# A graph layer on one core: TensorE's loop turned at another place, one more memset ahead of the left-over edges, and a dst block on another queue

## The chip, the core and the metric

The kernel runs on one core of a Trainium2 chip. The metric is the device time of one execution in microseconds. Five engines work side by side, each in the order of its own instruction list: TensorE (PE; the profile shows its weight loads as PEld), VectorE (DVE), ScalarE (ACT), GpSimd (POOL) and SyncE (SP). An engine waits for another one by semaphores only. SyncE, ScalarE and GpSimd also issue DMAs, each on a queue of its own; the transfers share 16 DMA engines.

## The reference

`x` has 12,500 nodes of 128 values, `edge_attr_48` 412,500 edges of 48 values, sorted by their destination `dst`. `src` and `batch` (all zeros) play no part in the result beyond one row of globals.

```python
h   = relu(layernorm(x))                                  # no scale, no shift
agg = segment_sum(edge_attr_48, dst, num_segments=12500)  # 48 values for a node
z   = concat([h, agg, graph_globals[0]])                  # 128 + 48 + 64
out = x + relu(z @ W1 + b1) @ W2 + b2                     # 256 hidden values
```

Everything is float32. Read and written in all: 79 MB of edges, 6.4 MB of x, 6.4 MB of result.

## The kernel before

**Edges into nodes.** The sorted edges are cut into chunks of 768 (128 partitions of 6 edges), and 4 chunks make a group. For a group VectorE builds one-hot tiles (`oh`: which of 28 neighbouring nodes an edge belongs to) and TensorE multiplies them with the edges (`su`, line 681), which gives the group's sums by node offset in a PSUM bank S0 or S1; ScalarE copies them out (`ss`, line 685). A second, wider one-hot (`pl`, 186 nodes, line 668) places them into the aggregate of 1,024 nodes in two PSUM banks (`pc`, line 703).

**Stages.** One iteration handles 11 groups of edges and 1,024 nodes; there are 12 iterations. The 11 groups lie in six slots: slots 0 to 3 and 5 hold two groups each, slot 4 one. Each slot has one buffer `e[s]` for its edges; once its sums are done, the loads for the next iteration (`le`, 576 KB for a group) go out on SyncE's queue, in the order of the sums. The nodes come in two blocks A and B of 512: x is loaded on ScalarE's queue (`lx`), VectorE computes the statistics (`st`, line 710), ScalarE normalizes (`xn`, line 731), TensorE transposes (`tu`, line 740), then come the first layer (`hh`, `ha`, lines 750 and 755), ScalarE's ReLU (`hi`, line 760) and, in the next iteration, the second layer (`w2`, line 776). VectorE adds the residual and keeps the result in SBUF (`ho` into `hold`, line 780), and only behind that does GpSimd compute x + b2 for the current block (`xb`, line 735), into the buffer that `ho` has just read. The load of the next x waits for `xb`, as it overwrites x.

**Order.** A class `Flow` collects all operations with the names that they read and write. From these names it derives the waits: an operation that writes a name waits for whoever wrote or read it before. On one engine the operations stand in the order in which the program lists them. TensorE's part of an iteration is, in order: sums of slots 0, 1, 2; placing of slot 5 (first half), 0 and 1; second layer of A and B; sums of slots 3, 4, 5; transposes; placing of slots 2, 3, 4 and 5 (second half); first layer. For TensorE alone the loop does not turn where an iteration begins, but ahead of the operation that `f.mark` names, here `su4`: between the sums of slots 3 and 4.

**Start.** SyncE issues the loads of the five blocks of `dst` (`ld`, lines 524 to 529; the last block has 25 full rows and one row that is filled by two small DMAs), then those of the first edges. ScalarE fills some buffers with zeros before it copies the transposed dst blocks (line 597).

**End.** After the loop, in `epilogue`, 5 full chunks and one of 84 edges are left over, and 212 nodes. `load_rest` puts the chunks into slot 0's buffer with two DMAs on SyncE's queue: `lez` (720 KB, writes the names `e0.0` and `e0.1`) and `lezt` (the 84 edges, 14 partitions; writes `e0.1` and `ezt`). Behind them on the same queue stand the 22 stores of the held results (`soh`, 256 KB each, line 786), then the stores of the last blocks A and of the left-over nodes; block B's last store is on ScalarE's queue. The left-over sums are `sur` (line 938), which for the chunk of 84 edges uses 14 rows only.

Of the kernel before, what the change touches and what calls it, by code (L numbers as in the profile page):

```python
# [18 lines left out]
P = 128  # L19
EPS = 1e-5  # L20
T = 6
CE = P * T
CG = 4
# [3 lines left out]
IN = 1024  # L27
# [7 lines left out]
V = 28  # L35
NV = 32
SLOTS = [(1, 6), (2, 7), (3, 8), (4, 9), (5,), (10, 11)]
NS = len(SLOTS)
# [367 lines left out]
def kernel(  # L406
# [12 lines left out]
    nc = tc.nc  # L419
    N, D = x.shape  # L420
    E, DE = edge_attr.shape
# [6 lines left out]
    TAIL = E - NFULL * CE  # L428
# [81 lines left out]
    op = f.op  # L510
    A, B, Z = 0, 1, 2

    def dma(eng, name, reads, writes, dst_ap, src_ap):
        def emit(i):
            with nc.allow_non_contiguous_dma(reason="small pieces"):
                return [f.of[eng].dma_start(dst_ap(i) if callable(dst_ap) else dst_ap, src_ap(i) if callable(src_ap) else src_ap)]  # L516
        op(eng, name, reads, writes, emit, dma=True)

    def load_dst(b):
        rows = min(P, NCH - b * P)  # L520
        full = min(P, NFULL - b * P)
        d = di[b]
        k = f"di{b}"
        dma("SP", f"ld{b}", [], [k], d[:full], dst[b * P * CE:(b * P + full) * CE].rearrange("(c e) -> c e", e=CE))
        if full < rows:
            n = CE // TAIL
            dma("SP", f"ld{b}r", [], [k + "r"], d[full:rows, :n * TAIL].rearrange("a (n e) -> a n e", e=TAIL),
                dst[None, None, E - TAIL:E].to_broadcast([1, n, TAIL]))
            dma("SP", f"ld{b}s", [], [k + "s"], d[full:rows, n * TAIL:], dst[None, E - TAIL:E - TAIL + CE - n * TAIL])

    def span(ap, i, a, n):
        return ap[ds(a(i), n)] if not isinstance(i, int) else ap[a(i):a(i) + n]
# [137 lines left out]
    def onehots(s):  # L670
        g = SLOTS[s]
        onehot(s, oh[s], ["rel_i"], rel_i[:, g[0] - 1:g[0]] if len(g) == 1 else rel_i[:, g[0] - 1:g[1]:g[1] - g[0]])
# [13 lines left out]

    def sums(s):
        m = len(SLOTS[s])
        add_up(s, s % 2, oh[s], e[s], ss[s], [f"e{s}.{j}" for j in range(m)], m * CG)

    def place(s, fresh=(), part=None):

# [36 lines left out]
    def norm(k, m=P):  # L729
        op("ACT", f"xn{k}", [f"x{k}", f"x{k}t", f"sc{k}", f"sh{k}"], [f"xn{k}"], lambda i: [  # L730
            nc.scalar.activation(xn[k][:m, r], xt[k][:m, r], AF.Relu, bias=sh[k][:m, r:r + 1], scale=sc[k][:m, r:r + 1]) for r in range(RR[k])])  # L731
# [56 lines left out]
    def prologue():  # L788
# [1 line left out]
        for b in range(NB):  # L790
            load_dst(b)
        dma("SP", "le5.1", [], ["e5.1"], e[5][:, CG:], edge_attr[:GE].rearrange("(c p t) d -> p c (t d)", p=P, t=T))
        for s in range(NS):
            if s == 2:
                load_x(A, lambda i: 0, eng="SP")
                load_x(B, lambda i: BN, eng="SP")
            for k in (0, 1):
                if (s, k) != (5, 1) and k < len(SLOTS[s]):
                    load_e(s, 1, k)
# [40 lines left out]
        for b in range(NB):  # L840
# [21 lines left out]
        places(1)  # L862
        op("DVE", "spare", [], ["spare"] + [f"di{b}" for b in range(NB)] + [f"di{NB - 1}r", f"di{NB - 1}s"] + [f"df{k}" for k in range(DF)],
           lambda i: [nc.vector.memset(hold[0][:, 0:1], 0.0)])
        for s in (3, 4, 5):
            onehots(s)
        for s in (2, 3, 4):
            places(s)
# [2 lines left out]
    def body(it):  # L871
        f.at = it

        def add_slots(*some):
            for s in some:
                sums(s)
                if it < NIT - 1:
                    load_e(s, 1)

        keep = lambda i: (i + NIT - 2) % (NIT - 1)  # L880
        farthest()
        fetch(1)
        add_slots(0, 1)
        for k in (A, B):
            stats(k)
            variance(k)
        add_slots(2)
        onehots(0)
        shift(A)
        shift(B)  # L890
        onehots(1)
        onehots(2)
        norm(A)
        norm(B)
        place(5, (0,), 0)
        place(0, (1,))
        place(1)
        places(5)
        fetch_off(1)
        places(0)  # L900
        places(1)
        for k in (A, B):
            second(k, P, ph[k], f"PH{k}", keep)
        for k in (A, B):
            add_b(k)

        add_slots(3, 4, 5)
        for s in (3, 4, 5):
            onehots(s)
        turn(A)  # L910
        turn(B, P, po, "PO")
        if it < NIT - 1:
            load_x(A, lambda i: (i + 1) % NIT * IN)
            load_x(B, lambda i: (i + 1) % NIT * IN + BN)
        for s in (2, 3, 4):
            place(s)
        place(5, (), 1)
        sums_out(A)
        sums_out(B)
        for s in (2, 3, 4):  # L920
            places(s)
        layers(layer_x)
        layers(layer_e)
        layers(relu)

    def epilogue():
        f.at = NIT
        m = RN // RZ
        load_rest()
        store_held()  # L930
        add_b(Z, m)
        stats(Z, m)
        variance(Z, m)
        shift(Z, m)
        norm(Z, m)
        rest = lambda j, c: P if j * CG + c < FULL else TP
        op("PE", "sur", ["oh0", "oh1", "e0.0", "e0.1", "ezt"], ["S0"], lambda i: [
            nc.tensor.matmul(S[0][NV * c:NV * c + V, j * DE:(j + 1) * DE], oh[j][:rest(j, c), c * T + t], e[0][:rest(j, c), j * CG + c, t * DE:(t + 1) * DE],  # L938
                             start=(t == 0), stop=(t == T - 1), skip_group_check=True)
            for j in range(2) for t in range(T) for c in range(min(CG, RC - j * CG))])  # L940
        op("ACT", "ssr", ["S0"], ["ssr"], lambda i: [nc.scalar.copy(ssr.rearrange("p j d -> p (j d)"), S[0][:, :2 * DE])])
        place(5, (0,), 0)
        turn(Z, m, S[1], "S1")
        verdict_0()
        verdict_1()
        todo = [(j,) + v for j, g in enumerate((1, 2)) for v in pieces(g)]
        op("PE", "pcr", ["ssr", "pl0", "pl1"], ["bk0"], lambda i: [
            nc.tensor.matmul(agg[bk][:DE, at:at + w], ssr[:, j], pl[j][:, 0, frm:frm + w], start=False, stop=True, skip_group_check=True)
            for j, bk, at, frm, w in todo])
        sums_out(Z, m)  # L950
        zr = [S[0][:, a * RN:(a + 1) * RN].rearrange("p (r c) -> p r c", r=RZ) for a in range(NH)]
        for a in range(NH):
            layer_x(f"z{a}", "S0", zr[a], Z, a, a == 0, m)
        for a in range(NH):
            layer_e(f"z{a}", "S0", zr[a], Z, a, m)
        for a in range(NH):
            relu(f"z{a}", "S0", zr[a], Z, a, m)
        second(A, P, ph[A], "PH0")
        store(A, lambda i: (i - 1) * IN)
        verdict_2()  # L960
        second(B, P, ph[B], "PH1")
        store(B, lambda i: (i - 1) * IN + BN, eng="ACT")
        second(Z, m, pt, "PT")
        store(Z, lambda i: i * IN, m)
        for e_ in f.of:
            op(e_, f"rb{e_}", ["bad"], [], lambda i, e_=e_: [f.of[e_].reg_load(flag_of[f.of[e_].engine], bad[0:1, 0:1])])
# [8 lines left out]
    ends = [f"ot{k}" for k in range(3)] + [f"x{k}" for k in (A, B)] + [f"hold{k}.{j}" for k in (A, B) for j in range(NIT - 1)]  # L975
    op("SP", "end", [], ends, lambda i: [nc.sync.nop(nofuse=True)])
    f.order((0, NIT - 1))
    f.mark = "su4"
    tc.mark_branch_hint_location("skip", engines=[ET.PE, ET.DVE])
    with tc.tile_critical(no_gpsimd_drain=True):  # L980
        f.run()
# [33 lines left out]
```

## Time and profile before

| | us |
|---|---|
| median of 3 runs | 277.77 (277.67 to 277.8) |
| the profiled execution | 277.39 |
| its span, first to last instruction | 275.6 |
| TensorE busy | 252.7 (92%) |
| VectorE busy | 239.5 (87%) |
| ScalarE busy | 128.2 (47%) |
| GpSimd busy | 54.5 (20%) |

The DMA moved 94.33 MB at a mean of 342 GB/s over the span.

How to read it: the span is shown in 40 equal slices of 6.9 us, and a digit is the busy share of a slice in tenths. A row of the timeline gives the start and the duration in us, the engine (a q behind it means that the engine only issues), the line of the kernel, the operation, the tile written and the tiles read, the shapes, how many instructions in a row it stands for, and in brackets how long the engine was idle before it and what ended that. A row of the windows gives the stretch, its length, then for PE, PEld, DVE, ACT and POOL busy time and number of instructions, and at the end TensorE's granted clock, the DMA's share and GB/s. A row of the DMA view gives tile written, tile read, queue, count, KB, and the us from issue to landing. A row of the waits gives who waited for what: us in total, times, the longest.

### The profile page before, as it was taken

The numbers are of one execution on the slowest core, as the hardware profiler recorded it, in microseconds if no ns is written. First come the engines' busy times: TensorE is split into PE (matmuls) and PEld (weight loads), VectorE is DVE, ScalarE is ACT, GpSimd is POOL, SyncE is SP. The second block draws the span as 40 slices with busy tenths as digits, with TensorE's granted clock in tenths as the row PEclk, the third lists the DMA queues.
The fourth block names the chain that finished last, engine by engine and source line by source line (L and its number), as shares of the span: only waits on it lengthen the run. The fifth ranks groups of instructions, "written<-read, shape, count | busy, mean of one in ns | idle before, by whom it ended". The sixth has DMA issues, their size and how long they took to land.

```text
span 275.6 us, 17205 instructions
## 1 busy us (share of the span) xinstructions
PE 252.7 (92%) x7567; PEld 195.6 (71%) x7568; DVE 239.5 (87%) x591; ACT 128.2 (47%) x316; POOL 54.5 (20%) x47
## 2 busy tenths in 40 slices
PE   2946999999999999999999999999999999999990
PEld 2946866867858849859768768578498497597580
DVE  4899997998989989989989979989899899799521
ACT  7800544535437337245445355373373463454520
POOL 8100050040220400500500502304105005007000
PEclk9955999999999999999999999999999999999999
DMA  6999999999999999999999999999999999995992
GB/s 213 297 363 356 341 357 362 356 357 361 356 361 357 356 362 356 356 362 356 356 362 356 356 362 356 359 359 356 362 357 356 362 356 356 362 356 208 368 363 73
DMA packets 79012, 94.33 MB, mean 342 GB/s; under 512 B 3227, under 2 KB 72189, under 8 KB 78998
## 3 DMA queue, kind: packets, MB, share of 16 engines
q1 hardware_dynamic: 75398, 87.63, 96.1%
q10 hardware_dynamic: 3312, 6.03, 6.2%
q0 software_dynamic: 288, 0.49, 0.7%
q8 instruction: 7, 0.11, 0.2%
q14 instruction: 7, 0.06, 0.1%
HBM read 87.75 MB, written 6.40 MB: 342 GB/s over the span
## 4 chain that ended last, share of the span: by engine, by line
PE 87%; SPq 5%; DMA 3%; issue 2%; DVE 0%
PE s L681 27%; PE ph L776 18%; PE ph L750 8%; PE ax L703 7%; SPq L516 5%; PE ph L755 5%; PE po L750 4%; PE pt L750 4%; PE pt L755 4%; DMA e<-in_edge_attr_dram 3%; PE ay L703 3%; PE pt L740 3%; PE po L740 2%; PE s L938 1%; PE s L750 0%
## 5 line engine op out<-in xcount | busy, mean ns | idle before, releaser
L662 DVE TENSOR_TENSOR oh<-iota_v,rel_i 128x1344 f32<-128x1344 f32 (+1 forms) x78 | 130.8, 1716 | 0.0
L681 PEld LDWEIGHTS s<-e,oh 128*28 128x28 f32 x6336 | 75.1, 109 | 23.3 <-issue 21.4
L681 PE MATMUL s<-e,oh 128*28 128x48 f32 x6336 | 80.9, 210 | 11.0 <-issue 6.7
L735 POOL TENSOR_TENSOR xba<-xa,b_sb 128x512 f32<-128x512 f32 x12 | 15.4, 1285 | 198.3 <-DVE holda L780 198.3
L685 ACT COPY ss<-s 128x96 f32<-128x96 f32 (+1 forms) x72 | 16.8, 234 | 70.6 <-PE s L681 70.6
L668 DVE TENSOR_SCALAR pl<-iota_w,off_i 128x186 f32<-128x186 f32 x141 | 35.1, 309 | 0.5
L735 POOL TENSOR_TENSOR xbb<-xb,b_sb 128x512 f32<-128x512 f32 x12 | 31.1, 2591 | 0.0
L760 ACT ACTIVATE hida<-ph,bias 128x512 f32<-128x512 f32 x12 | 8.2, 687 | 42.2 <-PE ph L755 42.2
L703 PE MATMUL ax<-pl,ss 128*48 128x186 f32 (+3 forms) x172 | 27.1, 300 | 0.0
L776 PEld LDWEIGHTS ph<-w,hida 128*128 128x128 f32 x208 | 24.2, 191 | 3.8 <-issue 3.8
L776 PE MATMUL ph<-w,hida 128*128 128x128 f32 x208 | 26.7, 281 | 0.0
L703 PE MATMUL ay<-pl,ss 128*48 128x186 f32 (+3 forms) x168 | 26.3, 297 | 0.0
L776 PE MATMUL ph<-w,hidb 128*128 128x128 f32 x208 | 25.6, 276 | 0.6 <-issue 0.6
L776 PEld LDWEIGHTS ph<-w,hidb 128*128 128x128 f32 x208 | 24.3, 192 | 0.8 <-issue 0.7
L731 ACT ACTIVATE xna<-xa,sha,sca 128x128 f32<-128x128 f32 x48 | 19.8, 482 | 5.1 <-DVE sha L727 5.1
L710 DVE BATCH_NORM_STATS2 sta<-xa 128x6 f32<-128x128 f32 x48 | 10.5, 281 | 12.1 <-DMA xa<-in_x_dram 12.1
L703 PEld LDWEIGHTS ax<-pl,ss 128*48 128x48 f32 x172 | 17.6, 126 | 4.3 <-issue 2.0
L731 ACT ACTIVATE xnb<-xb,shb,scb 128x128 f32<-128x128 f32 x48 | 19.6, 479 | 0.0
L703 PEld LDWEIGHTS ay<-pl,ss 128*48 128x48 f32 x168 | 17.8, 124 | 0.0
L755 PE MATMUL ph<-ags,w1a 48*128 48x512 f32 x48 | 13.5, 641 | 0.0
L750 PE MATMUL ph<-hta,w1h 128*128 128x512 f32 x24 | 13.5, 644 | 0.0
L750 PE MATMUL ph<-htb,w1h 128*128 128x512 f32 x24 | 12.3, 592 | 0.0
(150 smaller groups left out, 301.5 us busy)
## 6 DMA issues: line engine op xcount, KB each, us to landing
e<-in_edge_attr_dram SPq DMA_DIRECT2D x133, 576.0 KB, 10.0
xa<-in_x_dram ACTq DMA_DIRECT2D x11, 256.0 KB, 5.8
xb<-in_x_dram ACTq DMA_DIRECT2D x11, 256.0 KB, 6.3
out_dram<-holda SPq DMA_DIRECT2D x11, 256.0 KB, 3.2
out_dram<-holdb SPq DMA_DIRECT2D x11, 256.0 KB, 3.3
holda<-in_dst_dram SPq DMA_DIRECT2D x4, 384.0 KB, 4.9
e<-in_edge_attr_dram SPq DMA_DIRECT2D x1, 720.0 KB, 8.9
xa<-in_x_dram SPq DMA_DIRECT2D x1, 256.0 KB, 10.5
```

Of the source, the lines that this page charges most:

```text
L516: return [f.of[eng].dma_start(dst_ap(i) if callable(dst_ap) else dst_ap, src_ap(i) if callable(src_ap) else src_ap)]
L662: op("DVE", f"oh{name}", reads + ["iota_v"], [f"oh{name}"], lambda i: [nc.vector.tensor_tensor(ov, iota_v[:, None, None, :].to_broadcast([ ...
L668: nc.vector.tensor_scalar(out[:, j], iota_w, o[j], None, OP.is_equal) for j in range(len(o))])
L681: nc.tensor.matmul(S[k][NV * c:NV * c + V, j * DE:(j + 1) * DE], o[:, (j * CG + c) * T + t], ev[:, j * CG + c, t * DE:(t + 1) * DE], start ...
L685: op("ACT", f"ss{name}", [f"S{k}"], [f"ss{name}"], lambda i: [nc.scalar.copy(sv.rearrange("p j d -> p (j d)"), S[k][:, :m * DE])])
L703: out.append(nc.tensor.matmul(agg[bk][h:h + DE, at:at + w], sv[:, j], pv[:, j, frm:frm + w], start=bk in fresh and bk not in seen, stop=Tr ...
L731: nc.scalar.activation(xn[k][:m, r], xt[k][:m, r], AF.Relu, bias=sh[k][:m, r:r + 1], scale=sc[k][:m, r:r + 1]) for r in range(RR[k])])
L735: nc.gpsimd.tensor_tensor(xb[k][:m], xt[k][:m], b2_sb[:m, None, :].to_broadcast([m, RR[k], D]), OP.add)])
L740: op("PE", f"tu{k}", [f"xn{k}", "ident"], [key], lambda i: [nc.tensor.transpose(pv[:, r, :m], xn[k][:m, r], ident[:m, :m]) for r in range( ...
L750: nc.tensor.matmul(o, w1h[:, a * P:(a + 1) * P], hT[k][:, :, :m], start=first, stop=False, skip_group_check=True)])
L755: nc.tensor.matmul(o, w1a[h:h + DE, a * P:(a + 1) * P], ag[k // 2][h:h + DE, :, :m], start=False, stop=True, skip_group_check=True)])
L776: nc.tensor.matmul(ov[:m, r], hid[k][:, a, r, :m], w2[:, a], start=(a == 0), stop=(a == NH - 1)) for r in range(RR[k]) for a in range(NH)])
```

## The change

- In the loop the sums of slot 4 move from behind those of slot 3 into the first burst, behind slot 2; slot 3 takes S0 and slot 4 S1. The load of slot 4 for the next iteration and its one-hot move with it (and in the prologue the order of loads and one-hots follows). `f.mark` becomes `su3`, so that TensorE's loop turns behind the second layer, ahead of the sums of slot 3.
- The three DMAs of the last dst block are issued on ScalarE's queue instead of SyncE's.
- In the epilogue a memset `ezz` on GpSimd zeroes e[0]'s last chunk (128x288), listed ahead of `load_rest` and writing the name `e0.1`. The left-over sums then use all 128 rows for each chunk.
- In the epilogue the verdict on VectorE (a test whether the windows sufficed), the second layer of block A and its store move ahead, to just behind the left-over sums.

```diff
--- before.py
+++ after.py
@@ -521,12 +521,13 @@
         full = min(P, NFULL - b * P)
         d = di[b]
         k = f"di{b}"
-        dma("SP", f"ld{b}", [], [k], d[:full], dst[b * P * CE:(b * P + full) * CE].rearrange("(c e) -> c e", e=CE))
+        eng = "SP" if full == rows else "ACT"
+        dma(eng, f"ld{b}", [], [k], d[:full], dst[b * P * CE:(b * P + full) * CE].rearrange("(c e) -> c e", e=CE))
         if full < rows:
             n = CE // TAIL
-            dma("SP", f"ld{b}r", [], [k + "r"], d[full:rows, :n * TAIL].rearrange("a (n e) -> a n e", e=TAIL),
+            dma(eng, f"ld{b}r", [], [k + "r"], d[full:rows, :n * TAIL].rearrange("a (n e) -> a n e", e=TAIL),
                 dst[None, None, E - TAIL:E].to_broadcast([1, n, TAIL]))
-            dma("SP", f"ld{b}s", [], [k + "s"], d[full:rows, n * TAIL:], dst[None, E - TAIL:E - TAIL + CE - n * TAIL])
+            dma(eng, f"ld{b}s", [], [k + "s"], d[full:rows, n * TAIL:], dst[None, E - TAIL:E - TAIL + CE - n * TAIL])
 
     def span(ap, i, a, n):
         return ap[ds(a(i), n)] if not isinstance(i, int) else ap[a(i):a(i) + n]
@@ -686,7 +687,7 @@
 
     def sums(s):
         m = len(SLOTS[s])
-        add_up(s, s % 2, oh[s], e[s], ss[s], [f"e{s}.{j}" for j in range(m)], m * CG)
+        add_up(s, {3: 0, 4: 1}.get(s, s % 2), oh[s], e[s], ss[s], [f"e{s}.{j}" for j in range(m)], m * CG)
 
     def place(s, fresh=(), part=None):
 
@@ -790,7 +791,7 @@
         for b in range(NB):
             load_dst(b)
         dma("SP", "le5.1", [], ["e5.1"], e[5][:, CG:], edge_attr[:GE].rearrange("(c p t) d -> p c (t d)", p=P, t=T))
-        for s in range(NS):
+        for s in (0, 1, 2, 4, 3, 5):
             if s == 2:
                 load_x(A, lambda i: 0, eng="SP")
                 load_x(B, lambda i: BN, eng="SP")
@@ -862,7 +863,7 @@
         places(1)
         op("DVE", "spare", [], ["spare"] + [f"di{b}" for b in range(NB)] + [f"di{NB - 1}r", f"di{NB - 1}s"] + [f"df{k}" for k in range(DF)],
            lambda i: [nc.vector.memset(hold[0][:, 0:1], 0.0)])
-        for s in (3, 4, 5):
+        for s in (4, 3, 5):
             onehots(s)
         for s in (2, 3, 4):
             places(s)
@@ -884,12 +885,13 @@
         for k in (A, B):
             stats(k)
             variance(k)
-        add_slots(2)
+        add_slots(2, 4)
         onehots(0)
         shift(A)
         shift(B)
         onehots(1)
         onehots(2)
+        onehots(4)
         norm(A)
         norm(B)
         place(5, (0,), 0)
@@ -904,8 +906,8 @@
         for k in (A, B):
             add_b(k)
 
-        add_slots(3, 4, 5)
-        for s in (3, 4, 5):
+        add_slots(3, 5)
+        for s in (3, 5):
             onehots(s)
         turn(A)
         turn(B, P, po, "PO")
@@ -926,6 +928,7 @@
     def epilogue():
         f.at = NIT
         m = RN // RZ
+        op("POOL", "ezz", [], ["e0.1"], lambda i: [nc.gpsimd.memset(e[0][:, FULL], 0.0)])
         load_rest()
         store_held()
         add_b(Z, m)
@@ -933,16 +936,17 @@
         variance(Z, m)
         shift(Z, m)
         norm(Z, m)
-        rest = lambda j, c: P if j * CG + c < FULL else TP
         op("PE", "sur", ["oh0", "oh1", "e0.0", "e0.1", "ezt"], ["S0"], lambda i: [
-            nc.tensor.matmul(S[0][NV * c:NV * c + V, j * DE:(j + 1) * DE], oh[j][:rest(j, c), c * T + t], e[0][:rest(j, c), j * CG + c, t * DE:(t + 1) * DE],
+            nc.tensor.matmul(S[0][NV * c:NV * c + V, j * DE:(j + 1) * DE], oh[j][:, c * T + t], e[0][:, j * CG + c, t * DE:(t + 1) * DE],
                              start=(t == 0), stop=(t == T - 1), skip_group_check=True)
             for j in range(2) for t in range(T) for c in range(min(CG, RC - j * CG))])
         op("ACT", "ssr", ["S0"], ["ssr"], lambda i: [nc.scalar.copy(ssr.rearrange("p j d -> p (j d)"), S[0][:, :2 * DE])])
+        verdict_0()
+        verdict_1()
+        second(A, P, ph[A], "PH0")
+        store(A, lambda i: (i - 1) * IN)
         place(5, (0,), 0)
         turn(Z, m, S[1], "S1")
-        verdict_0()
-        verdict_1()
         todo = [(j,) + v for j, g in enumerate((1, 2)) for v in pieces(g)]
         op("PE", "pcr", ["ssr", "pl0", "pl1"], ["bk0"], lambda i: [
             nc.tensor.matmul(agg[bk][:DE, at:at + w], ssr[:, j], pl[j][:, 0, frm:frm + w], start=False, stop=True, skip_group_check=True)
@@ -955,8 +959,6 @@
             layer_e(f"z{a}", "S0", zr[a], Z, a, m)
         for a in range(NH):
             relu(f"z{a}", "S0", zr[a], Z, a, m)
-        second(A, P, ph[A], "PH0")
-        store(A, lambda i: (i - 1) * IN)
         verdict_2()
         second(B, P, ph[B], "PH1")
         store(B, lambda i: (i - 1) * IN + BN, eng="ACT")
@@ -975,7 +977,7 @@
     ends = [f"ot{k}" for k in range(3)] + [f"x{k}" for k in (A, B)] + [f"hold{k}.{j}" for k in (A, B) for j in range(NIT - 1)]
     op("SP", "end", [], ends, lambda i: [nc.sync.nop(nofuse=True)])
     f.order((0, NIT - 1))
-    f.mark = "su4"
+    f.mark = "su3"
     tc.mark_branch_hint_location("skip", engines=[ET.PE, ET.DVE])
     with tc.tile_critical(no_gpsimd_drain=True):
         f.run()
```

## The prediction

> **What bounds the kernel now.** I read the page first: shares, slices, the chain.
>
> ```profile
> span 275.6 us, 17205 instructions
> PE 252.7 (92%) x7567; PEld 195.6 (71%) x7568; DVE 239.5 (87%) x591; ACT 128.2 (47%) x316; POOL 54.5 (20%) x47
> DMA  6999999999999999999999999999999999995992
> PE 87%; SPq 5%; DMA 3%; issue 2%; DVE 0%
> ```
>
> TensorE is busy nearly always and the chain runs along it, but the DMA row stands at 9 too, with one dip at slice 36. So two things are nearly full, and the first question is which of them paces the loop. The timeline of TensorE and the windows say:
>
> ```profile
> 35.15 1.73 PE L681 MATMUL s<-e,oh 128*28 128x48 f32 x144 [0.42 <-issue]
> 209.77 1.73 PE L681 MATMUL s<-e,oh 128*28 128x48 f32 x144 [0.40 <-issue]
> 248.89 1.73 PE L681 MATMUL s<-e,oh 128*28 128x48 f32 x144 [0.41 <-issue]
> 219.26:238.84 19.58, 19.09 (x615) 14.56 (x613) 18.00 (x45) 9.50 (x25) 3.84 (x2) 1.00 1.09 358
> ```
>
> The three rows are the sums of slots 4 and 5, just behind TensorE's loop turn, whose price is the bracket: 0.40 to 0.42 us. From 35.15 to 209.77 lie nine iterations, 19.40 us each; from 209.77 to 248.89 two, 19.56 each. In the last column the DMA moves 358 GB/s. Now the loads, by SyncE's issues and the DMA view's time to landing for each:
>
> ```profile
> 220.12 1.41 SPq L516 DMA_DIRECT2D e<-in_edge_attr_dram  x1
> e<-in_edge_attr_dram SPq DMA_DIRECT2D x1, 576.0 KB, 9.6
> 239.44 1.92 SPq L516 DMA_DIRECT2D e<-in_edge_attr_dram  x1
> e<-in_edge_attr_dram SPq DMA_DIRECT2D x1, 576.0 KB, 9.8
> ```
>
> These are the last load of an iteration, twice: they land at 229.7 and 249.2, 19.5 apart. Slot 5's sums, a third into the burst at 248.89, begin near 249.5. So the loads, each with some 10 us of queue ahead of it, run at 19.5 to 19.6, TensorE by itself at 19.4, and TensorE has by the end used up its lead. The stream of loads sets when the last edges are there; what follows them sets the rest. That rest, on SyncE's queue (waits, timeline, DMA):
>
> ```profile
> 242.25 0.72 SPq L516 DMA_DIRECT2D e<-in_edge_attr_dram  x1
> e<-in_edge_attr_dram SPq DMA_DIRECT2D x1, 720.0 KB, 8.9
> SPq L516 <- DMA e<-in_edge_attr_dram: 8.2, 1, 8.2
> 251.22 0.36 SPq L516 DMA_DIRECT2D e<-in_edge_attr_dram  x1
> 251.62 0.37 SPq L516 DMA_DIRECT2D out_dram<-holda  x1
> ...
> 265.67 0.64 SPq L516 DMA_DIRECT2D out_dram<-holdb  x1
> out_dram<-holdb SPq DMA_DIRECT2D x1, 256.0 KB, 3.3
> 269.93 0.77 SPq L516 DMA_DIRECT2D out_dram<-otr  x2
> out_dram<-otr SPq DMA_DIRECT2D x1, 96.0 KB, 1.9
> ```
>
> The left-over edges (`lez`, 720 KB) are issued at 242.25, as soon as slot 0's last sums have let go of e[0]. The small tail load (`lezt`) writes the same key, so it waits until `lez` has landed: the 8.2 us, which makes the dip. Behind it, in order, stand the 22 held stores: first issue 251.62, last landing 265.67 + 3.3 = 269.0, so 17.35 us in all, about 0.73 each. The last store of all, of the left-over nodes, lands at 269.93 + 1.9 = 271.8. The end thus has two tracks, TensorE's and SyncE's, and SyncE's has under 3 us of slack.
>
> **The change, part by part.**
>
> *The memset of e[0]'s last chunk on GpSimd.* `ezz` stands ahead of `lez` in the list and writes the key `e0.1`; `lez` writes it too. So `lez` now waits for GpSimd, and GpSimd works in order: behind the last iteration's two residual additions, which wait for VectorE's held sums.
>
> ```profile
> 247.76 0.69 DVE L780 TENSOR_TENSOR holda<-ph,xba 128x512 f32 x1
> 249.77 2.59 POOL L735 TENSOR_TENSOR xbb<-xb,b_sb 128x512 f32<-128x512 f32 x1
> 7.67 0.31 POOL L820 MEMSET rel<- 128x228 f32 x1
> 11.03 0.85 DVE L662 TENSOR_TENSOR oh<-iota_v,rel 128x672 f32<-128x672 f32 x1
> holda<-in_dst_dram SPq DMA_DIRECT2D x1, 384.0 KB, 3.1
> 258.45 2.87 PE s L938 x72
> ```
>
> The second addition ends at 252.36 today. Slot 4's one-hot now stands ahead of the held sums on VectorE: one more instruction of 0.85 us, 0.8 as they overlap; 253.15. The memset is 128x288, the nearest row 0.31 for 128x228: 0.35 (bounds 0.3 and 0.5); `lez` goes at 253.5 instead of 242.25. By then the DMA is empty. The nearest row for a load into an empty queue is the first dst block: 3.1 us for 384 KB, of which 1.1 is data at 358 GB/s, so 2.0 of latency; 720 KB then take 2.0 + 2.1 = 4.1 (bounds: 3.6, with the shorter latency of the last store, 1.9 us less 0.3 for its 96 KB; 5.8, if all of the 3.1 grew with size). Landed 257.6; `lezt` and the first store 0.4 later, as from 251.22 to 251.62: 258.0. That is 6.4 us behind today's 251.62. Seventeen and a third us on, the held stores have landed: 275.4. Behind them now lie the three last stores, 256 + 256 + 106 KB at the same rate, 0.73 + 0.73 + 0.3: 277.1 against 271.8, **+5.3 us**.
>
> [...]
>
> On TensorE the left-over sums wait for `lezt`: 258.0 + 2.0 = 260.0 against 258.45 today, 1.5 us. Its chain then ends near 271, six us ahead of the stores: nothing. The same holds for the second layer of block A and its store moved up in the epilogue: on SyncE that store still stands behind the 22. ScalarE's copy and the verdict gain or lose nothing that ends last.
>
> *Left-over sums with all rows.* Twelve of the 72 matmuls go from 14 to 128 rows. Both kinds are in one group:
>
> ```profile
> L938 PE MATMUL s<-e,oh x72: 201/206/227, 258.4 to 261.1; 128*28 128x48 f32 x60, 14*28 14x48 f32 x12
> ```
>
> 202 to 227 ns whatever the rows: 0.
>
> *Last dst block on ScalarE's queue.* Three issues leave SyncE's front, and the edge loads behind them go earlier by as much. What that is worth is what the DMA leaves free there:
>
> ```profile
> 5.00:6.00 1.00, 0.82 (x4) 0.82 (x5) 0.62 (x3) 0.64 (x2) 1.00 (x3) 1.00 0.81 255
> 6.00:7.00 1.00, 1.00 (x7) 1.00 (x6) 0.42 (x2) 0.46 (x1) 1.00 (x2) 1.00 0.87 314
> 7.00:8.00 1.00, 1.00 (x7) 1.00 (x7) 0.27 (x2) 1.00 (x2) 0.97 (x3) 1.00 0.71 209
> 8.00:9.00 1.00, 1.00 (x6) 0.64 (x5) 0.71 (x3) 0.95 (x3) 0.00 (x0) 1.00 0.89 193
> 16.90 2.14 PE L681 MATMUL s<-e,oh 128*28 128x48 f32 x96 [2.49 <-DMA e<-in_edge_attr_dram]
> 6.54 0.85 ACT L597 COPY rel<-pt 128x384 f32<-128x384 f32 x1 [0.90 <-PE pt L596]
> ```
>
> Below 358 GB/s lie 103 + 44 + 149 + 165 KB, 1.3 us of the stream. Bounds 0 (small pieces fill those microseconds whoever issues them) and 1.3; I take half, **-0.65 us**, and as the whole loop hangs on the stream, all of it arrives at the end. ScalarE issues three DMAs more before its first work; 0.9 us of idle time ahead of its first dst copy takes half of that, and the first sums, which wait 2.49 us for edges, the rest.
>
> *Slot 4 in the first burst, the turn behind the second layer.* The same matmuls and one-hots in another order. The turn's 0.4 us may go, since behind 128-column matmuls more work is pending than behind sums of 12 ns; but TensorE then only waits for loads sooner. Slot 4's load is also moved ahead of slot 3's, so it is there first. Bounds: 0 and rival F below; I take 0. ScalarE's small copy of slot 4's sums now stands ahead of the normalization, whose result TensorE needs only behind the whole second layer and slots 3 and 5: cover enough. SyncE's order of loads follows that of the sums; no issue is added.
>
> **Sum:** +5.3 - 0.65 = +4.6 on the profiled execution, 277.39 us with its 275.6 span: 282.0. That execution is 0.4 below the median of the runs, 277.77, so **282.4 us**.
>
> **The rivals.**
>
> *S, a second ring closes.* The later held sums make the additions later, and block B's load of x waits for them on ScalarE.
>
> ```profile
> 239.65 0.86 DVE L710 BATCH_NORM_STATS2 stb<-xb 128x6 f32<-128x128 f32 x4
> 230.25 2.59 POOL L735 TENSOR_TENSOR xbb<-xb,b_sb 128x512 f32<-128x512 f32 x1
> 232.95 0.34 ACTq L516 DMA_DIRECT2D xb<-in_x_dram  x1
> xa<-in_x_dram ACTq DMA_DIRECT2D x1, 256.0 KB, 5.7
> xb<-in_x_dram ACTq DMA_DIRECT2D x1, 256.0 KB, 6.5
> ```
>
> Round the ring: statistics of B to held sums 8.1 (239.65 to 247.76), to the end of the additions 4.6, to the issue 0.1 (232.84 to 232.95), to landing 6.5: 19.3. With 0.8 more it is 20.1 and over the loads' 19.56: 0.55 in each of 11 iterations, 6 us more, **288.4 us**. (Behind that issue on ScalarE stand the copies of the aggregate; TensorE has eight matmuls of the first layer to do before it needs them.) Against it: B takes 6.5 where A takes 5.7 because it is issued half a us behind A; issued 0.8 later it should land in 5.7, and the ring is 19.3 again.
>
> *F, faster: TensorE paces the loop after all.* If the loads run at 19.5 only because TensorE lets go of buffers at that pace, the turn's 0.4 comes off, 19.0 an iteration instead of 19.4 to 19.56: 5.2 us over the loop and 5.3 + 0.65 as above, 277.77 + 5.3 - 0.65 - 5.2 = **277.2**, just faster. It decides where the last loads of successive iterations land under 19.1 apart. For it: the gap is real, and nothing else stops TensorE. Against it: the loads' 10 us of queue and 358 GB/s in each slice. [...] The trace shows only today's gap.
>
> *N, no change:* the additions are early enough that `lez` is hidden. Today's slack is 271.8 - 269.0 less 1.76 for the stores that line up behind, 1 us; so the first held store may go at 252.6 and `lez` at 248.1, when the sums at 247.76 have only begun and both additions are still to come. Then only the start's gain and some of the tail's remain: 277.5.
>
> **How the numbers follow.** Forecast 0.78, S 0.12, F 0.06, N 0.04. The forecast's own bounds: start 0 to 1.3, `lez` 3.6 to 5.8, a memset slowed beside VectorE, a ring of S that bites in some iterations only (up to 2 us): 280.8 to 285.2. That leaves out S, F and N, 0.22, and so the low end goes a little down: 280.5 to 285.5. 0.2% is about what a measurement tells from no change: F is half on either side of it (0.03 faster), N too (0.02), the rest is slower.
>
> **What would show it.** SyncE's one wait ahead of the left-over load ends with GpSimd's memset near 253; first held store near 258, last landing near 275, DMA idle for 5 us near 250; TensorE's chain ends before them. Right or wrong for the start: the first edge load's issue near 2.9. For S: VectorE's wait for x of block B grows from iteration to iteration. For F: iterations of 19.0. The forecast is wrong if the left-over load is issued near 242 or if the stores aren't what ends last.

## The result and the profile after

The changed kernel takes 285.28 us, the median of its runs (284.78 to 285.82), against 277.72 us for the kernel before beside it: a ratio of 1.0275, 95% interval 1.0249 to 1.0301. The forecast was 282.4 us with a range of 280.5 to 285.5, slower with a chance of 0.9. On the two profiled executions the loss is 284.78 - 277.39 = 7.4 us where +4.6 was forecast. So the sign and the place are right, and 2.8 us more are to be explained.

The page of the changed kernel: span, busy times, the DMA's row in 40 slices of 7.1 us, and the engines' shares of the chain that ended last.

```profile
span 282.9 us, 17192 instructions
PE 254.0 (90%) x7567; PEld 198.6 (70%) x7568; DVE 238.7 (84%) x591; ACT 128.5 (45%) x316; POOL 54.1 (19%) x48
DMA  6999999999999999999999999999999999904993
DVE 37%; DMA 29%; POOL 12%; PE 9%; issue 6%; SPq 2%; POOLq 0%; ACT 0%; DVEq 0%; ACTq 0%
```

Two things are new. The DMA row has a 0, a slice in which next to nothing moves, where the kernel before had a 5. And the chain that ended last has left TensorE: 87% of it lay there before, 9% now, while VectorE, the transfers and GpSimd carry 78%. The timeline around the end says how they are linked:

```profile
250.39 0.69 DVE L781 TENSOR_TENSOR holda<-ph,xba 128x512 f32 x1
...
252.39 2.58 POOL L736 TENSOR_TENSOR xbb<-xb,b_sb 128x512 f32<-128x512 f32 x1
254.91 0.34 POOL L931 MEMSET e<- 128x288 f32 x1
...
255.27 4.79 SPq L516 DMA_DIRECT2D e<-in_edge_attr_dram  x2
260.11 0.36 SPq L516 DMA_DIRECT2D out_dram<-holda  x1
...
272.40 0.42 DVE L779 TENSOR_TENSOR otr<-pt,xbr 106x256 f32<-106x256 f32 x1 [0.18 <-PE pt L777]
...
275.22 0.48 SPq L516 DMA_DIRECT2D out_dram<-ota  x1
275.75 1.79 SPq L516 DMA_DIRECT2D out_dram<-otr  x2
```

Held sums of block A, second residual addition, memset `ezz`, `lez` at 255.27, the first held store at 260.11, the last issues near 277: the chain that the prediction drew, each link behind the one before. The row of VectorE at 272.40 is the end of TensorE's track, the result of the left-over nodes: it is there at 272.82, and its store is issued from 275.75 on, behind the others. So the queue of stores ends last, and not TensorE. SyncE's longest wait, in the view of the waits, is the first of the two long ones:

```profile
SPq L516 <- POOL e L931: 13.2, 1, 13.2
```

And the DMA view of the same kernel has the second:

```profile
e<-in_edge_attr_dram SPq DMA_DIRECT2D x1, 720.0 KB, 4.4
```

SyncE stands 13.2 us for the memset, and then for the 4.4 us in which `lez` crosses a DMA that stood empty (8 GB/s in the slice with the 0). What differs from the forecast is when it all starts: the held sums of the last iteration are at 250.39, against 247.76 before and about 248.6 in the forecast.

### The profile page after: what moved, and what is told of

It is laid out like the page before. It is cut to its first block, busy times and chain, and to the rows that moved or that the text cites. A ratio compares the mean times of both kernels' runs of the same rounds, so it can differ in the third digit from the quotient of the medians.

```text
span 282.9 us, 17192 instructions
## 1 busy us (share of the span) xinstructions
PE 254.0 (90%) x7567; PEld 198.6 (70%) x7568; DVE 238.7 (84%) x591; ACT 128.5 (45%) x316; POOL 54.1 (19%) x48
## 4 chain that ended last, share of the span: by engine, by line
DVE 37%; DMA 29%; POOL 12%; PE 9%; issue 6%; SPq 2%; POOLq 0%; ACT 0%; DVEq 0%; ACTq 0%
DMA xb<-in_x_dram 21%; DVE oh L663 20%; POOL xbb L736 10%; DMA e<-in_edge_attr_dram 6%; DVE pl L669 5%; DVE stb L711 3%; PE ph L777 3%; PE s L682 3%; DVE holda L781 2%; SPq L516 2%; POOL xba L736 2%; DMA xa<-in_x_dram 2%; DVE off_i L656 1%; DVE smb L720 1%; DVE smb L716 1%
## 5 line engine op out<-in xcount | busy, mean ns | idle before, releaser
L663 DVE TENSOR_TENSOR oh<-iota_v,rel_i 128x1344 f32<-128x1344 f32 x78 | 129.0, 1694 | 0.5 <-PE s L682 0.5
L682 PEld LDWEIGHTS s<-e,oh 128*28 128x28 f32 x6336 | 74.6, 109 | 19.1 <-issue 17.1
L682 PE MATMUL s<-e,oh 128*28 128x48 f32 x6336 | 79.1, 210 | 8.0 <-issue 5.7
L686 ACT COPY ss<-s 128x96 f32<-128x96 f32 x72 | 15.8, 231 | 52.6 <-PE s L682 52.3
L736 POOL TENSOR_TENSOR xbb<-xb,b_sb 128x512 f32<-128x512 f32 x12 | 29.7, 2475 | 0.4 <-DVE holdb L781 0.4
L777 PE MATMUL ph<-w,hida 128*128 128x128 f32 x208 | 27.6, 287 | 0.0
L777 PEld LDWEIGHTS ph<-w,hida 128*128 128x128 f32 x208 | 25.1, 198 | 3.5 <-issue 3.4
L747 ACT COPY ags<-ax 48x512 f32<-48x512 f32 x12 | 7.0, 580 | 33.0 <-POOL xbb L736 32.1
L732 ACT ACTIVATE xnb<-xb,shb,scb 128x128 f32<-128x128 f32 x48 | 19.6, 479 | 0.0
L711 DVE BATCH_NORM_STATS2 stb<-xb 128x6 f32<-128x128 f32 x48 | 10.4, 280 | 9.7 <-DMA xb<-in_x_dram 9.7
L756 PE MATMUL ph<-ags,w1a 48*128 48x512 f32 x48 | 17.5, 641 | 0.0
```

The lines of the kernel that those rows point to most:

```text
L663: op("DVE", f"oh{name}", reads + ["iota_v"], [f"oh{name}"], lambda i: [nc.vector.tensor_tensor(ov, iota_v[:, None, None, :].to_broadcast([ ...
L682: nc.tensor.matmul(S[k][NV * c:NV * c + V, j * DE:(j + 1) * DE], o[:, (j * CG + c) * T + t], ev[:, j * CG + c, t * DE:(t + 1) * DE], start ...
L686: op("ACT", f"ss{name}", [f"S{k}"], [f"ss{name}"], lambda i: [nc.scalar.copy(sv.rearrange("p j d -> p (j d)"), S[k][:, :m * DE])])
L711: op("DVE", f"st{k}", [f"x{k}", f"x{k}t"], [f"st{k}"], lambda i: [nc.vector.bn_stats(st[k][:m, r], xt[k][:m, r]) for r in range(RR[k])])
L736: nc.gpsimd.tensor_tensor(xb[k][:m], xt[k][:m], b2_sb[:m, None, :].to_broadcast([m, RR[k], D]), OP.add)])
L756: nc.tensor.matmul(o, w1a[h:h + DE, a * P:(a + 1) * P], ag[k // 2][h:h + DE, :, :m], start=False, stop=True, skip_group_check=True)])
```

## The experiments

The kernel before took 277.76 us beside the first four runs below, 278.12 beside the version that came out best, and 278.03 beside the other four.

### The memset and all rows taken out of the change

```diff
-        op("POOL", "ezz", [], ["e0.1"], lambda i: [nc.gpsimd.memset(e[0][:, FULL], 0.0)])
         load_rest()
...
+        rest = lambda j, c: P if j * CG + c < FULL else TP
...
-            nc.tensor.matmul(..., oh[j][:, c * T + t], e[0][:, j * CG + c, ...],
+            nc.tensor.matmul(..., oh[j][:rest(j, c), c * T + t], e[0][:rest(j, c), j * CG + c, ...],
```

> The changed kernel with the memset and the full rows undone (everything else stays). Theory W (the left-over load's wait for GpSimd is what the tail pays): the left-over load goes again near 242 and the end is TensorE's, whose transposes in the last iteration stood at 250.3 against 250.55 in the kernel before: 277.0 to 277.6 us. Rival L (the loop's new order itself costs the time, by VectorE's later held sums): 282 us or more.

Measured: 278.27 us, ratio 1.0015 (0.9994 to 1.0036). The rival that puts the loss into the loop falls: without the memset the new order costs nothing that can be measured. It doesn't gain either, and the time is 0.7 us over what was expected. And its held sums come no earlier than in the changed kernel (250.39), by its timeline:

```profile
251.39 0.68 DVE L781 TENSOR_TENSOR holda<-ph,xba 128x512 f32 x1
...
235.31 16.84 SPq L516 DMA_DIRECT2D e<-in_edge_attr_dram  x5
252.19 0.36 SPq L516 DMA_DIRECT2D out_dram<-holda  x1
```

The first held store goes out at 252.19, 0.6 us behind the 251.62 of the kernel before, at once behind the last issue of edges, which ends at 252.15 and waits for GpSimd no longer. So late held sums are harmless as long as SyncE's queue doesn't hang on GpSimd.

### The memset and all rows alone

```diff
+        op("POOL", "ezz", [], ["e0.1"], lambda i: [nc.gpsimd.memset(e[0][:, FULL], 0.0)])
         load_rest()
...
-            nc.tensor.matmul(..., oh[j][:rest(j, c), c * T + t], e[0][:rest(j, c), j * CG + c, ...],
+            nc.tensor.matmul(..., oh[j][:, c * T + t], e[0][:, j * CG + c, ...],
```

> The kernel before with only the memset and the full rows. Theory W: the additions on GpSimd end at 252.4 as before, the memset near 252.7, the left-over load lands 4.4 later and the first held store goes near 257.6, 2.5 sooner than the 260.1 of the changed kernel: 282.0 to 282.6 us. Rival L: 277.7 us.

Measured: 282.71 us, ratio 1.0163 (1.0137 to 1.0189), +4.95 us. That is the main term of the sum by itself (+5.3), and 0.1 over what was expected here. Its timeline around the end:

```profile
253.51 0.34 POOL L929 MEMSET e<- 128x288 f32 x1
...
253.88 4.75 SPq L516 DMA_DIRECT2D e<-in_edge_attr_dram  x2
258.68 0.37 SPq L516 DMA_DIRECT2D out_dram<-holda  x1
...
259.99 1.21 PE L938 MATMUL s<-e,oh 128*28 128x48 f32 x72 [0.57 <-DMA e<-in_edge_attr_dram]
```

The two runs don't add up: +0.5 without the memset and +4.95 with it alone make 5.5, and together they cost 7.6 (285.28 - 277.72). The new loop has a cost that only shows when the memset is there to pass it on.

### Slot 4's one-hot back behind the held sums

```diff
-        onehots(4)
         norm(A)
...
-        for s in (3, 5):
+        for s in (4, 3, 5):
             onehots(s)
```

> The changed kernel with slot 4's one-hot moved back behind the held sums on VectorE. Theory R (a late start in iteration 0 goes round the ring of held sums, additions, load of x for B, statistics, at 19.25 us a turn, and is kept): the ring is 0.8 shorter, 18.5, the lag of 2.6 is worked off in three or four iterations, the additions end near 252.6 and the time is 282.1 to 282.7 us. Rival P (the one-hot merely stands in front, no ring): only its own 0.8 us goes: 284.2 to 284.6 us.

Measured: 282.04 us, ratio 1.0159 (1.0134 to 1.0183): 3.2 us less than the changed kernel, for one instruction of 0.85 us that stands some places later. The held sums of block A in iterations 1 and 11, by the timeline, and VectorE's largest entry in the view of the waits tell why. The timeline of the kernel before (iteration 11, 247.76, stands in the prediction):

```profile
53.69 0.68 DVE L780 TENSOR_TENSOR holda<-ph,xba 128x512 f32 x1
```

The timeline of the changed kernel (iteration 11, 250.39, stands above):

```profile
57.07 0.68 DVE L781 TENSOR_TENSOR holda<-ph,xba 128x512 f32 x1
```

With the one-hot back:

```profile
57.11 0.69 DVE L781 TENSOR_TENSOR holda<-ph,xba 128x512 f32 x1
247.17 0.68 DVE L781 TENSOR_TENSOR holda<-ph,xba 128x512 f32 x1
```

The waits of the changed kernel:

```profile
DVE stb L711 <- DMA xb<-in_x_dram: 9.7, 10, 1.2
```

And with the one-hot back:

```profile
DVE sta L711 <- DMA xa<-in_x_dram: 8.7, 11, 1.9
```

Both changed kernels are 3.4 us late in iteration 1, though only one of them has the one-hot ahead. With the one-hot back the first iteration happened to be later by as much: in it TensorE's transposes stand at 40.08 instead of 39.32, and block A's second layer, at 33.75, took 2.39 us instead of 2.05. From there to iteration 11 an iteration takes on average (247.17 - 57.11) / 10 = 19.01 us with the one-hot back and (250.39 - 57.07) / 10 = 19.33 with it ahead; the kernel before takes (247.76 - 53.69) / 10 = 19.41. So the one catches up all of its lag, 4 us, and the other 0.7 of it. What holds the other up is VectorE's wait for x of block B, about 1 us in each of ten iterations: the ring of rival S (statistics, held sums, GpSimd's additions, load of x) is closed, at 19.33. It doesn't lose in each iteration, as S had it; it keeps the kernel from making good a delay of the start. In the changed kernel block B's x is issued at 235.76, right behind its addition (233.14 + 2.58). VectorE's wait for x of block A in the other kernel is no such ring: that load is issued at 231.83, 2 us behind its addition (228.49 + 1.29), so there is room in it.

Not all of the 3.2 us is the ring's. The second addition takes 1.90 us with the one-hot back (249.18 to 251.08) and 2.58 in the changed kernel, 0.7 us; why it is shorter is open.

### TensorE's turn alone

```diff
-    f.mark = "su4"
+    f.mark = "su3"
```

> The kernel before with only the place of the turn moved, to ahead of slot 3's sums. Theory S (the stream of loads sets the end of the loop): the gap of 0.4 us goes or shrinks, and the time stays within 0.5 us of 277.7. Rival F (TensorE paces the loop): 272.5 to 274 us.

Measured: 277.65 us, ratio 0.9994 (0.9977 to 1.0012). In the first iterations the gap is gone: the sums of slots 3, 4 and 5 stand in one piece, the first row below, and come again at 54.52, 18.86 us later, where the kernel before takes 19.4. Later a gap is there again, 0.34 us at 151.73 and 0.35 at 249.59, at another place, ahead of slot 5's sums and 144 matmuls behind the turn. TensorE's timeline:

```profile
35.66 2.81 PE L681 MATMUL s<-e,oh 128*28 128x48 f32 x240
...
151.73 1.22 PE L681 MATMUL s<-e,oh 128*28 128x48 f32 x96 [0.34 <-issue]
249.59 1.22 PE L681 MATMUL s<-e,oh 128*28 128x48 f32 x96 [0.35 <-issue]
```

From 151.73 to 249.59 lie five iterations of 19.57 us, the pace at which the prediction saw the loads land. So TensorE without the gap would go round in 18.9 us, and once it has used up its lead the loads hold it to theirs. Rival F falls. That the late gap is the wait for slot 5's edges fits this pace, but the profile calls it "issue" and names no load.

### Where the lag of the start comes from

This is read from the traces of these runs; the one edit that aimed at it, further below, settles nothing. In the first pass through the loop TensorE stops twice for nothing but its own instructions ("issue"). The kernel before, the rest of its slot 1, the rest of its second layer and its transposes:

```profile
24.23 0.32 PE L681 MATMUL s<-e,oh 128*28 128x48 f32 x2 [1.73 <-issue]
...
31.63 1.94 PE L776 MATMUL ph<-w,hidb 128*128 128x128 f32 x15 [0.56 <-issue]
...
36.82 0.66 PE L740 MATMUL pt<-ident,xna 128*128 128x128 f32 x4
```

The changed kernel, its sums of slots 1, 2 and 4, and its transposes:

```profile
23.41 1.28 PE L682 MATMUL s<-e,oh 128*28 128x48 f32 x50 [2.17 <-issue]
24.89 1.62 PE L682 MATMUL s<-e,oh 128*28 128x48 f32 x77 [0.20 <-DMA e<-in_edge_attr_dram]
30.07 1.65 PE L682 MATMUL s<-e,oh 128*28 128x48 f32 x67 [3.56 <-issue]
39.32 0.66 PE L741 MATMUL pt<-ident,xna 128*128 128x128 f32 x4
```

The turn alone, its slots 0, 1 and 2:

```profile
16.67 1.22 PE L681 MATMUL s<-e,oh 128*28 128x48 f32 x95 [0.66 <-DMA e<-in_edge_attr_dram]
21.20 2.38 PE L681 MATMUL s<-e,oh 128*28 128x48 f32 x97 [3.31 <-issue]
25.40 0.85 PE L681 MATMUL s<-e,oh 128*28 128x48 f32 x29 [1.81 <-DMA e<-in_edge_attr_dram]
27.92 1.65 PE L681 MATMUL s<-e,oh 128*28 128x48 f32 x67 [1.67 <-issue]
```

Count the matmuls between the two stops: 50 + 77 = 127 and 97 + 29 = 126; in the kernel before 2, the 96 of slot 2, 12 of placing and 17 of the second layer, 127. With its weight load each is two instructions (the page counts 7567 matmuls and 7568 weight loads), so the stops are 252 to 254 of them apart, whatever the work. And they move with the code ahead of them. What lies behind the mark stands first in TensorE's loop and is jumped over in the first pass: slots 4 and 5 before (144 matmuls), 3 and 5 in the changed kernel (192, 48 more), 3, 4 and 5 with the turn alone (240, 96 more). The first stop comes after 94 matmuls of slot 1 in the kernel before, after 96 - 50 = 46 of them in the changed kernel (48 earlier), after 95 of slot 0 with the turn alone (95 earlier). So the stops hang on the place of an instruction in the code and not on any tile; I read them as TensorE waiting for its program. The DMA view fits this. It has a queue of the kind "instruction", and on it one packet of 0.02 MB starts ahead of each of the four resumptions of the kernel before (at 21.66 and 28.98 us) and of the changed kernel (at 20.76 and 27.45), 2.57 to 2.65 us ahead. The second one in the kernel before (window 28.6 to 30) and in the changed kernel (27 to 28.6):

```profile
q8 instruction: 1, 0.02, 5.1%
q8 instruction: 1, 0.02, 4.5%
```

By these rows, from one resumption to the next are 7.4 us before (24.23 to 31.63), 6.7 in the changed kernel (23.41 to 30.07) and 6.7 with the turn alone (21.20 to 27.92), all three while the DMA is full of edges (312 to 358 GB/s in the windows of 2 us of the first two, 359 with the turn alone in its two windows, 20 to 23.4 and 27 to 28.6). What lies between then decides the exposed wait. In the kernel before that is placing and block A's second layer, long instructions (2.05 us for 16 matmuls), and 0.56 us is left to wait; in the changed kernel it is sums alone (2.90 us for 127), and 3.56 is left. The transposes of the first iteration are so at 39.32 instead of 36.82, 2.5 us late, and the held sums of the next one another 0.85 later for the one-hot: the 3.4 us at 57.07. The start differs between executions, by up to 1.6 us with the same loop: these transposes stand at 36.8 to 38.4 in the five profiles with the loop and turn of the kernel before, and at 39.3 to 40.6 in the four with slot 4's sums in the first burst.

### The 84 edges in a tile of their own

If the memset costs by what it makes wait, it may stay if nothing waits for it: the 84 edges get a tile `ez`, zeroed and loaded in the prologue, `lezt` goes from the end, and the left-over sums use all rows. This into the changed kernel, with slot 4's one-hot back behind the held sums as above:

```diff
+    ez = const.tile([P, T * DE], F32)
...
-        dma("SP", "lezt", [], ["e0.1", "ezt"], e[0][:TP, FULL], edge_attr[E - TAIL:E]...)
...
+        pool("ezz", ["ezt"], lambda: nc.gpsimd.memset(ez, 0.0))
+        dma("SP", "lezt", [], ["ezt"], ez[:TP], edge_attr[E - TAIL:E]...)
...
-        op("POOL", "ezz", [], ["e0.1"], lambda i: [nc.gpsimd.memset(e[0][:, FULL], 0.0)])
...
-            nc.tensor.matmul(..., e[0][:, j * CG + c, t * DE:(t + 1) * DE],
+            nc.tensor.matmul(..., (e[0][:, j * CG + c] if j * CG + c < FULL else ez)[:, t * DE:(t + 1) * DE],
```

> The changed kernel with slot 4's one-hot behind the held sums and with the 84 left-over edges in a tile of their own, zeroed and loaded in the prologue: no memset in the epilogue, no wait of one left-over load for the other, full rows kept. Theory W+C (waits on SyncE's queue were all that the tail lost, and full rows save TensorE 1.7 us): stores start behind the left-over load from 243 on, TensorE's chain ends the kernel and ends 2.2 us sooner than in the kernel before: 275.0 to 276.0 us. Rival (TensorE's end does not matter, or the stores in the loop's last microseconds hold the last edges up): 277.5 us or more.

Measured: 276.61 us, ratio 0.9928 (0.9897 to 0.9959): faster than both kernels, by less than was expected. Is it the tile, the loop or the epilogue's order? The tile alone, in the kernel before, by the same lines:

```diff
+    ez = const.tile([P, T * DE], F32)
...
-            nc.tensor.matmul(..., oh[j][:rest(j, c), c * T + t], e[0][:rest(j, c), j * CG + c, ...],
+            nc.tensor.matmul(..., oh[j][:, c * T + t], (e[0][:, j * CG + c] if j * CG + c < FULL else ez)[...],
```

> The kernel before with only the tile of its own and full rows. Theory C (sums with 14 rows among sums with 128 rows cost about 0.1 us each time the rows change): the left-over sums take 1.2 us instead of 2.9 at full clock, and the kernel 275.8 to 276.3 us. The prediction's step (rows cost nothing): 277.7 us.

Measured: 278.24 us, ratio 0.9999 (0.9968 to 1.0029). A miss. The sums did get short, 1.14 us up to the next work instead of 2.9, but TensorE's timeline shows a new wait behind them:

```profile
258.60 0.74 PE L939 MATMUL s<-e,oh 128*28 128x48 f32 x49
...
259.74 0.53 PE L703 MATMUL ax<-pl,ss 128*48 128x140 f32 x4
261.80 0.40 PE L740 MATMUL s<-ident,xnr 106*128 106x106 f32 x2 [1.54 <-ACT xnr L731]
```

The transposes of the left-over nodes wait 1.54 us for ScalarE's normalization; the kernel before had them at 261.7 too, behind its longer sums. What is needed is other work at that place, and the changed epilogue has it: block A's second layer. So the tile and that order, with the loop and the start of the kernel before:

```diff
         op("ACT", "ssr", ["S0"], ["ssr"], ...)
+        verdict_0()
+        verdict_1()
+        second(A, P, ph[A], "PH0")
+        store(A, lambda i: (i - 1) * IN)
         place(5, (0,), 0)
         turn(Z, m, S[1], "S1")
-        verdict_0()
-        verdict_1()
...
-        second(A, P, ph[A], "PH0")
-        store(A, lambda i: (i - 1) * IN)
```

> The kernel before (its loop, its start) with the left-over edges in a tile of their own, full rows, and the changed kernel's order of the epilogue: verdict, second layer of A and its store right behind the left-over sums. Theory T (with SyncE's waits gone the end is TensorE's; the saved 1.7 us of the left-over sums count only if TensorE has other work while ScalarE normalizes the left-over nodes, and the loop's order is worth nothing): TensorE ends near 267.7 instead of 269.4, 275.9 to 276.6 us, like the kernel with the changed loop and a tile of its own. Rival (it was the changed loop that won there): 277.5 us or more.

Measured: 276.31 us, ratio 0.9924 (0.9891 to 0.9956), the lowest median, and no different from the one with the changed loop. Its timeline at the end:

```profile
242.86 0.72 SPq L517 DMA_DIRECT2D e<-in_edge_attr_dram  x1
243.62 1.97 SPq L517 DMA_DIRECT2D out_dram<-holda  x1
...
260.46 2.05 PE L776 MATMUL ph<-w,hida 128*128 128x128 f32 x16
262.44 0.53 PE L703 MATMUL ax<-pl,ss 128*48 128x140 f32 x4
262.90 0.40 PE L740 MATMUL s<-ident,xnr 106*128 106x106 f32 x2
```

The held stores go out at 243.62, at once behind the last load, and TensorE has no wait in front of the left-over transposes. Of the whole change two parts are worth something, and only together: the epilogue's order and the full rows. The rows without the order are the run above with 278.24 us; the order without the rows is the run without the memset, 278.27, which has the changed loop besides.

### Slot 4 between the two halves of the second layer

Were the code's stop in the changed kernel to fall behind longer instructions, its lag should shrink. So slot 4's sums and one-hot were moved behind block A's second layer:

```diff
-        add_slots(2, 4)
+        add_slots(2)
...
-        onehots(4)
...
+        second(A, P, ph[A], "PH0", keep, "PE")
+        add_slots(4)
+        onehots(4)
...
-        for k in (A, B):
-            second(k, P, ph[k], f"PH{k}", keep)
+        second(A, P, ph[A], "PH0", keep, "DVE")
+        second(B, P, ph[B], "PH1", keep)
```

> The changed kernel with slot 4's sums not in the first burst but between the two halves of the second layer; one-hot, turn, memset as changed. Theory I (TensorE's code block arrives too late in iteration 0 because the first burst is longer, and the late start goes round the ring): the gap of 3.6 us shrinks under 1.5, transposes of iteration 0 near 37.5 instead of 39.3, additions end near 253.5 instead of 255.0: 283.3 to 284.2 us. Rival P (the ring is 0.8 longer, that alone makes the lag): 285.0 to 285.6 us.

Measured: 287.03 us, ratio 1.0301 (1.0241 to 1.036): slower still, a miss. Its timeline:

```profile
24.79 1.28 PE L682 MATMUL s<-e,oh 128*28 128x48 f32 x50 [2.17 <-issue]
30.54 0.68 PE L682 MATMUL s<-e,oh 128*28 128x48 f32 x19 [1.73 <-issue]
...
36.49 0.86 DVE L663 TENSOR_TENSOR oh<-iota_v,rel_i 128x672 f32<-128x672 f32 x1 [2.77 <-PE s L682]
```

The stops stay in the sums, since the code ahead of them is as long as before (46 matmuls into slot 1, then 50 + 77), and a wait of 2.77 us is new: VectorE's one-hot for slot 4 now waits for TensorE's sums, ahead of the held sums. The edit added a cost of its own and so can't say what the stop is worth.

### The last dst block alone

```diff
-        dma("SP", f"ld{b}", ...
+        eng = "SP" if full == rows else "ACT"
+        dma(eng, f"ld{b}", ...
```

The same for the two small DMAs behind it.

> The kernel before with only the last dst block on ScalarE's queue. The changed kernel's trace has the stream of loads 0.3 us earlier at its end: 277.2 to 277.6 us. The prediction's step had 0.65: 277.1. Rival (ScalarE's later copies of dst delay VectorE's one-hots, 0.9 us at its first x): 278.0 to 278.6 us.

Measured: 278.47 us, ratio 1.0006 (0.9974 to 1.0037). No gain of 0.65 us can be seen; the interval reaches from -0.7 to +1.0 us. The median lies where the rival has it (ScalarE's later copies of `dst`), but this interval doesn't decide between them.

## Why the prediction was right and where it was not

- *The memset's wait, +5.3 us.* Right, place and size: 4.95 us by itself. SyncE waits for GpSimd, the DMA runs dry, the held stores start late and end last. From the first held store to the last landing 19.1 us were said (258.0 to 277.1); here 260.11 to about 279.0 is 18.9.
- *"0.8 as they overlap; 253.15" for the end of the second addition.* This is the step that failed: 254.97 (252.39 + 2.58), 1.8 us later. Only the one-hot's own 0.8 us was counted as delay of the held sums. There are 2.5 us of delay from the first iteration besides, of which the ring gives back 0.7 by the end.
- *"Slot 4 in the first burst [...] I take 0", "cover enough".* The costs that were weighed, in the steady loop, are nothing indeed. The first pass was not looked at, where this step puts fast instructions between two waits for code.
- *`lez` takes 4.1 us.* It took 4.4, inside the bounds; 0.3 more.
- *"[...] behind 128-column matmuls more work is pending".* This was an estimate, and no run shows what is pending. What the turn alone shows is that behind the second layer the gap of 0.4 us is gone in the first iterations (the row at 35.66), and that one of 0.34 to 0.35 us is there later at another place.
- *The start, -0.65 us.* The first edge load does go out at 2.89 instead of 4.67, but no gain reached the end: the last store hangs on the ring and the memset, not on the stream of edges, so a gain of the stream is not a term of that sum. This, the 1.8 and the 0.3 are 2.75 of the 2.8 us.
- *All rows: "0".* Wrong, with no effect here. The 72 sums take 1.21 us with all rows (memset alone) and took 2.94 mixed. The group's row showed durations of 201 to 227 ns for both kinds, and a duration is not the distance to the next; the row's own starts, 258.4 to 261.1 for 72 matmuls, would have shown it. In the changed kernel TensorE isn't last, so the 1.7 us were lost; in the best version they count.
- *Rival S* was right about the ring; its period is the 19.3 of the argument against S (x of B lands in 5.8 us there, 6.3 before), and what the ring does is to keep the delay, not to add to it. *Rival F* was right that TensorE without the gap goes round faster (18.9 us) and wrong that the loop would follow: the loads hold it at 19.6. *Rival N* fell with the memset alone.

## What to carry to other kernels

Before a cheap instruction is put ahead of a transfer, ask on which engine it stands and what stands before it there: 0.34 us of memset cost 5 us because GpSimd came to it late and 22 stores were queued behind the load. A delay of the first iteration may be made good later or stay to the end. To tell, compare the period of each ring with the pace of the loop: a ring only a little under that pace (here 19.33 against 19.57 us) carries the delay to the end. And do a memset for a partial chunk where engines are idle, in a tile that no one else writes.

## What the runs showed of the hardware

**The number of rows.** Of the left-over sums the last 12 matmuls of the program alternate between 128 and 14 rows in the kernel before; in float32 the profile shows each of them as two, so 24 of the 72. TensorE's timeline of the kernel before:

```profile
258.38 2.94 PE L938 MATMUL s<-e,oh 128*28 128x48 f32 x72
```

Against 1.21 us with all rows, quoted above for the memset alone, that is 1.73 us more for 11 changes of rows, some 0.16 us for each. With the tile of its own the same 24 alternate between two tiles at 128 rows each, and all 72 take 1.14 up to the next work: it is the mix of rows that costs, not the change of tile. Whether 14 rows alone, without the mix, would be slow wasn't run.

**The clock after a pause.** In the changed kernel TensorE waits 3.17 us for the left-over edges. Its timeline:

```profile
261.36 1.88 PE L940 MATMUL s<-e,oh 128*28 128x48 f32 x72 [3.17 <-DMA e<-in_edge_attr_dram]
263.17 2.96 PE L777 MATMUL ph<-w,hida 128*128 128x128 f32 x16
```

And its windows there, where the third number from the end is the granted clock:

```profile
262.00:264.00 2.00, 2.00 (x44) 1.88 (x36) 0.00 (x0) 0.24 (x1) 0.00 (x0) 0.50 1.04 381
264.00:266.00 2.00, 2.00 (x14) 1.94 (x13) 0.00 (x0) 0.00 (x0) 0.00 (x0) 0.73 1.00 370
```

Behind the 3.17 us of waiting the granted clock is 0.50 from 262 to 264 and 0.73 in the next two us, and the sums take 1.88 us instead of 1.21, block A's second layer 2.96 instead of 2.05 (best version). With the memset alone TensorE waits 0.90 us ahead of the left-over transposes at 262.56, and its granted clock is 1.00 in each window from 262 to 270.

**Waiting for code.** The first pass through the loop's code stopped TensorE twice in the kernel before, the changed kernel and the turn alone, 252 to 254 matmuls and weight loads apart, for 0.56 to 3.56 us, with the DMA at 312 to 359 GB/s. That it waits for code is read from where the stops fall and from the instruction packets ahead of four of them. The shortest of these stops had long instructions ahead of it, the longest sums alone.
